# Moving the mode sums of a Fourier mixing to GpSimd, storing its modes in pairs, and asking for the next stage's first data before them

## The chip, the cores and the metric

The kernel runs on one core of one Trainium2 chip. The metric is the time that the device takes for one launch, in microseconds (us). The kernel before was run three times: 11272.87, 11274.17 and 11285.87 us, median 11274.17 us. A profiler recorded one more execution, whose own time was 11293.58 us.

A core has five engines that run at the same time, each through its own list of instructions: TensorE (PE, matrix products), VectorE (DVE), ScalarE (ACT), GpSimd (POOL) and SyncE (SP, which here only starts transfers). Sixteen DMA engines move data between the main memory (DRAM) and the on-chip memory (SBUF). PE writes its results to a second on-chip memory (PSUM). An instruction that needs the result of another engine or of a transfer waits for a semaphore, and everything behind it on its own engine waits with it.

## The reference

64 images of 256x256 points and 64 texts of 77x256 numbers are the inputs. A tokenizer made of four Fourier layers turns each image into 256x256 numbers, these 256 rows and the 77 text rows make 333 tokens, and a transformer block with a routed feed-forward part works on them. Cut to what matters here:

```python
h = concatenate([x, gx, gy]) ; v = h @ p_w + p_b            # 32 channels
for i in range(4):
    x_ft = rfft2(v)
    out1 = einsum('bixy,ioxy->boxy', x_ft[:, :, :12, :12],  W1)   # low modes
    out2 = einsum('bixy,ioxy->boxy', x_ft[:, :, -12:, :12], W2)   # mirrored low modes
    x1 = irfft2(out_ft holding out1 and out2)
    v = x1 + einsum('bcxy,cd->bdxy', v, w_w[i]) + w_b[i]
    v = (v - mean) * rsqrt(var + 1e-5) * bn_g[i] + bn_b[i]        # over images and points
    if i < 3: v = relu(v)
h = einsum('bcxy,cu->bxyu', v, q_w) + q_b                   # 256 x 256 per image
h = concatenate([h, txt])                                   # 333 tokens
h = h + attention(layernorm(h))
h = h + routed_ffn(layernorm(h))                            # the better half of the tokens
```

Only 24 x 12 complex modes of each channel are kept. The multiplication of these modes by W1 and W2 is called mixing below. The kernel takes the sum and the sum of squares for the normalisation from the modes, so it needs sums of products of modes over all images before it can scale anything.

## The kernel before, in words

The program goes through these stages, in the profile's time: the transform of the input (`forward_first`, to about 115 us), mixing 0 with its statistics, layer 0 (to about 2540), mixing 1 (its loop from about 2560 to 2606), layer 1, mixing 2, layer 2, mixing 3 (its loop ends at about 8645), and the transformer, image by image, to the end. The function `mix` (from L427) does a mixing and its statistics; `layer` (from L551) turns the mixed modes of every image back into points, adds the channel product, applies the normalisation and transforms the result forward again. The order in which a layer's steps are issued is written out by hand in `ORDER`: words such as `pre5` or `ld2@1`, where the number is the step's index and `@1` means that the step is done for one image ahead. Mixing and layers run under a manual schedule: each engine executes its instructions in the order in which the program issues them.

**Mixing.** The loop runs over 12 values of kp. Each step handles two of the 24 x-modes for all 64 images; the images lie on 64 partitions, twice (the two modes, kk = 0 and 1). PE makes 48 small products (L457) into a PSUM tile; ACT copies it out as `e` (L469). From `e`, ACT (L474, L475) and DVE (L476, L477) fill `ob`, one of three buffers of 128 partitions with the modes in the order in which they will be read; DVE copies a slice to `f0` (L478), forms combinations in `a_` (two L480), multiplies by `e` (L486) and adds the product to the accumulator `acc` (L487; the first step writes `acc` directly, L484). ACT makes two small copies of 64 partitions into `fr` (L494), which holds the modes in mirrored order. SP then stores each half of `ob` with a transfer of 512 KB over 64 partitions (L495) to `mix_d`, which in DRAM has the index order image, part, mode, channel: an image's modes are one contiguous piece.

**Statistics.** After the loop DVE reduces `acc` (L502 to L504), combines `fr` with `f0` (L505 to L507: difference, sum, product), reduces that (L508 to L511), PE sums over partitions (L513), and small operations, with a square root on ACT (L523), give the scale `s_` and the shift `t_` (L518 to L530).

**Start of a layer.** DVE prepares the constant rows of two tiles `ams` (L584, L590). SP then loads into them the mixed modes of the first two images (`load_am`, L623, four transfers). POOL multiplies them by the scale (`scale_am`, L631), PE expands them in x (L662), DVE transposes (L670), PE expands in y into `ring` (L682), and in layers 1 and 2 adds the channel product of the layer's input `vin` (L693), which SP loads in the steps `ld` (L656, two transfers of 512 KB per `vin`, four `vin` buffers). In layer 0 there is no `vin`: its input is the tile `mv`, which holds a grid, loaded by SP (L598, two transfers of 2 MB, each behind nothing but the stores of mixing 0), and rows of `x`, loaded by POOL (`load_x`, L638), which must come after the grid. In the program's order, `load_am` for two images comes first, then (in layer 0) the x loads, then `scale_am`, then the steps of `ORDER`, the first of which in layers 1 and 2 issue `ld`.

**Start of the transformer.** Constants come from a table (`cstt`, on SP's queue) and weights on ACT's queue (from L872: w1, w2, then the four attention weights). A few products of weights (L922 to L947) are made once. Then each image runs through `image_rows`: load the modes of the image (`am`), scale and reduce (L964, L968), expand (L970, L975), load the last layer's points in eight transfers of 1 MB (`ch`, pool `inp` of seven buffers) and reduce them over channels on PE (L982). This part is not under the manual schedule: a scheduler orders it, and may move it beside the end of mixing 3. The pool `inp` is made after the pool of constants, `tcon`.

Of the kernel before, what the change touches and what calls it, by code (L numbers as in the profile page):

```python
# [9 lines left out]
F32 = mybir.dt.float32  # L10
# [7 lines left out]
C = 32  # L18
M = 12
# [134 lines left out]
def tile_fno_fusion_transformer(ctx: ExitStack, tc: tile.TileContext, a, cst_d, grid_d, out):  # L154
# [27 lines left out]

    vd = [dram.tile([128, 8, 8, S], F32, name=f"v{b}_{n}") for n in range(2) for b in range(B)]
    vd = [vd[:B], vd[B:]]
    mix_d = [dram.tile([B, 2, KX, 32 * C], F32, name=f"mix{i}") for i in range(L)]
    xh_d = [dram.tile([128, B, 144], F32, name=f"xh{i}") for i in range(1, L)]

    flip = [0]
# [239 lines left out]
    def mix(i, lhs, wm, u2, spread):  # L428
# [5 lines left out]
        with tc.tile_pool(name="mo", bufs=1) as op, tc.tile_pool(name="me", bufs=3) as ep, \  # L434
# [13 lines left out]
            for kp in range(M):  # L448
# [19 lines left out]
                for hv in halves:  # L468
                    nc.scalar.copy(  # L469
                        e[hv].rearrange("p g q s o -> p q g (s o)"),  # L470
                        ps[hv, :, 0:384].rearrange("p q (g s) -> p q g s", g=3),
                    )
                    ev = e[hv].rearrange("p g q s o -> p (g q) s o")
                    nc.scalar.mul(o1[hv, 0], ev[:, :, 2, :], -1.0)  # L474
                    nc.scalar.copy(o1[hv, 1], ev[:, :, 1, :])  # L475
                    nc.vector.tensor_copy(o0[hv, 0], ev[:, :, 1, :])  # L476
                    nc.vector.tensor_copy(o0[hv, 1], ev[:, :, 2, :])  # L477
                    nc.vector.tensor_copy(f0[hv, kp], ev[:, 0, 1:3, :])  # L478
                    for n, (us, fs) in enumerate(((0, 1), (3, 2))):
                        nc.vector.scalar_tensor_tensor(  # L480
                            a_[hv, :, n, :], ev[:, :, us, :], 2.0, ev[:, :, fs, :], ALU.mult, ALU.add
                        )
                    if kp == 0:
                        nc.vector.tensor_mul(acc[hv], a_[hv], ev[:, :, 1:3, :])  # L484
                    else:
                        nc.vector.tensor_mul(a_[hv], a_[hv], ev[:, :, 1:3, :])  # L486
                        nc.vector.tensor_add(acc[hv], acc[hv], a_[hv])  # L487
                if kp == 0:
                    nc.vector.tensor_add(fin[0:B, 1, :], e[0:B, 0, 0, 1, :], e[0:B, 0, 0, 0, :])
                for kk in range(2):  # L490
                    to = (M - kp) % M if kk == 0 else M - 1 - kp
                    hv = slice(64 * kk, 64 * kk + B)
                    if kk or kp != M // 2:
                        nc.scalar.copy(fr[hv, to], e[hv, 0, 0, 1:3, :])  # L494
                    nc.sync.dma_start(  # L495
                        mix_d[i][:, :, 2 * kp + kk, :], ob[kp % NB][hv].rearrange("b p o k -> b p (o k)")
                    )
            for hv in halves:
                q = fin[hv, 0, :]
                t1 = op.tile([128, C], F32, name="t1", bufs=2)  # L500
                t2 = op.tile([128, C], F32, name="t2", bufs=2)
                nc.vector.reduce_sum(q, acc[hv].rearrange("p a s o -> p o (a s)"), axis=AX.X)  # L502
                nc.vector.tensor_add(t1[hv], acc[hv, 0, 0, :], acc[hv, 0, 1, :])
                nc.vector.scalar_tensor_tensor(q, q, 2.0, t1[hv], ALU.mult, ALU.subtract)  # L504
                nc.vector.tensor_sub(fr[hv, :, 0, :], fr[hv, :, 0, :], f0[hv, :, 0, :])  # L505
                nc.vector.tensor_add(fr[hv, :, 1, :], fr[hv, :, 1, :], f0[hv, :, 1, :])
                nc.vector.tensor_mul(fr[hv], fr[hv], f0[hv])  # L507
                nc.vector.reduce_sum(t1[hv], fr[hv, :, 0, :].rearrange("p a o -> p o a"), axis=AX.X)  # L508
                nc.vector.reduce_sum(t2[hv], fr[hv, :, 1, :].rearrange("p a o -> p o a"), axis=AX.X)
                nc.vector.tensor_sub(t1[hv], t1[hv], t2[hv])  # L510
                nc.vector.scalar_tensor_tensor(q, t1[hv], 0.5, q, ALU.mult, ALU.add)  # L511
# [34 lines left out]
    def layer(i, st, src, dst, acc):  # L546
# [7 lines left out]
        with ExitStack() as cx:  # L554
# [66 lines left out]
            def load_am(b):  # L621
                for n in range(2):
                    nc.sync.dma_start(  # L623
                        ams[b % 2][64 * n:64 * n + 2 * KX],
                        mix_d[i][b].rearrange("p k c -> (p k) c")[:, 512 * n:512 * n + 512],
                    )

            def scale_am(b):
# [21 lines left out]
                    load_x(b, n)  # L650

            def ld(b, t, e):
                vin[b, t] = ip.tile([128, 8, S], F32, name="vin")
                for n in range(2):
                    rows = slice(4 * n, 4 * n + 4)
                    nc.sync.dma_start(vin[b, t][:, rows], src[b][:, t, rows])  # L656
# [153 lines left out]
            for word in ORDER[min(i, 1)].split():  # L810
# [2 lines left out]
                name = word if word in run else word.rstrip("0123456789")  # L813
                steps.append((run[name], int(word[len(name):] or 0), e, int(late or 0)))

            for b in range(2):
                load_am(b)
            if i == 0:
# [42 lines left out]

    src = vd[L % 2]
    s_, t_ = st
    tcon = ctx.enter_context(tc.tile_pool(name="tcon", bufs=1))
    inp = ctx.enter_context(tc.tile_pool(name="inp", bufs=7))
    tabt = tables(tcon, "exT", "tri", "cstt")
    EXT, MASK4, IOTA = tabt("exT"), tabt("mask4"), tabt("iota")
    TRI = tabt("tri").rearrange("p (t j) -> p t j", t=3)
# [90 lines left out]

    def image_rows(b):  # L960
        am = ap_.tile([2 * KX, 32 * C], F32, name="am")
        nc.sync.dma_start(am, mix_d[L - 1][b].rearrange("p k c -> (p k) c"))
        tmp = am.rearrange("p (o k) -> p o k", k=32)
        nc.vector.tensor_tensor(  # L964
            tmp, tmp, qrow[0:2 * KX].to_broadcast([2 * KX, C, 32]), ALU.mult
# [268 lines left out]
```

## Time and profile before

| what | value |
|---|---|
| three runs, median | 11274.17 us |
| profiled execution, its own time | 11293.58 us |
| span of the profiled execution | 11291.7 us |
| busy share of the span: PE, DVE, ACT, POOL | 94%, 75%, 57%, 13% |
| transfers | 3457.29 MB, 306 GB/s mean |
| stores of modes (L495) | 96 of 512 KB, 5.6 us to landing (median) |
| loop of mixing 1, 2560 to 2604 us | DVE busy 41.86 us, ACT 39.35, PE 21.74, POOL 0 |

Busy times say how long an engine had an instruction in work, not whether the end of the program waited for it. For that the profile has a chain of waits: it starts from the last instruction and goes back, at each step, to what released it. A line of a group gives the line of the kernel, the engine, the operation, the tiles written and read with their shapes, then the count, total busy time and mean time of one, and then how long the engine stood idle before such instructions and what ended the wait. "issue" stands for time in which an engine waited for nothing that the profile shows.

### The profile page before, as it was taken

How to read it: one execution, taken by the hardware profiler on the slowest of the kernel's cores; microseconds unless marked ns; L12 is line 12 of the kernel's file. 1: busy time of each engine (PE TensorE's matmuls, PEld its weight loads, DVE VectorE, ACT ScalarE, POOL GpSimd, SP SyncE). 2: the span in 40 equal slices, each digit the busy share in tenths (PEclk: the TensorE clock that was granted, in tenths of full speed). 3: DMA queues.
4: the chain of work that ended last, by engine and by line, in shares of the span. 5: the costliest groups of instructions: out<-in, count | busy, mean ns of one | idle time of the engine just before them, and what ended most of it. 6: DMA issues, size and time to landing. Idle time of an engine off the chain costs nothing.

```text
span 11291.7 us, 409300 instructions
## 1 busy us (share of the span) xinstructions
PE 10625.0 (94%) x182550; PEld 5738.0 (51%) x182550; DVE 8446.5 (75%) x10381; ACT 6473.1 (57%) x10673; POOL 1442.4 (13%) x2179
## 2 busy tenths in 40 slices
PE   6999999998999999999799999999996999999999
PEld 3555555554444444444444444444443666666666
DVE  6888888887777777777677777777775666666665
ACT  5777777775566655566555566655563333333333
POOL 1111111110000000000000000000000333333333
PEclk8999999998999999999899999999998999999999
DMA  6776676678999999999899999999998555555553
GB/s 213 247 250 244 249 247 248 246 253 320 383 376 382 380 377 372 374 379 379 305 375 380 380 376 378 381 380 376 372 379 291 226 227 228 227 227 228 226 227 140
DMA packets 972544, 3457.29 MB, mean 306 GB/s; under 512 B 149784, under 2 KB 199320, under 8 KB 903832
## 3 DMA queue, kind: packets, MB, share of 16 engines
q1 hardware_dynamic: 905344, 3366.80, 77.8%
q0 software_dynamic: 58288, 60.60, 2.3%
q8 instruction: 1428, 23.40, 0.8%
q10 hardware_dynamic: 7144, 3.72, 0.1%
q14 instruction: 340, 2.79, 0.1%
HBM read 1733.60 MB, written 1696.92 MB: 304 GB/s over the span
## 4 chain that ended last, share of the span: by engine, by line
PE 62%; DMA 20%; DVE 9%; ACT 3%; issue 3%; SPq 2%; POOL 0%; ACTq 0%; DVEq 0%; POOLq 0%
PE ring L752 15%; DMA v<-vo 11%; PE ring L682 9%; PE ring L730 8%; DMA vin<-v 6%; PE ring L693 5%; PE hp L982 4%; PE ring L662 3%; PE pp L1145 3%; PE pp L1156 3%; PE ring L786 2%; DVE vo L707 2%; PE pp L1110 2%; PE pp L1175 2%; PE pp L1072 1%
## 5 line engine op out<-in xcount | busy, mean ns | idle before, releaser
L741 ACT ACTIVATE ring<-ring 128x1024 f32<-128x1024 f32 x3072 | 3115.8, 1014 | 1188.4 <-PE ring L730 1119.5
L719 DVE STREAM_TRANSPOSE t<-vo 128x2048 f32<-128x2048 f32 x1536 | 3465.7, 2286 | 20.9 <-DVE vo L707 0.9
L730 PE MATMUL ring<-vo,w 32*32 32x512 f32 x49152 | 2413.1, 600 | 85.0 <-ACT vo L705 68.3
L707 DVE TENSOR_SCALAR vo<-ring 128x1024 f32<-128x1024 f32 x1280 | 1544.5, 1221 | 1199.7 <-PE ring L693 806.6
L705 ACT ACTIVATE vo<-ring 128x1024 f32<-128x1024 f32 x1792 | 1791.7, 1023 | 1044.1 <-PE ring L693 500.9
L752 PE MATMUL ring<-t,cst 32*32 32x512 f32 x49152 | 2072.0, 599 | 51.0 <-issue 44.9
L752 PEld LDWEIGHTS ring<-t,cst 32*32 32x32 f32 x49152 | 913.4, 103 | 925.6 <-issue 622.6
L730 PEld LDWEIGHTS ring<-vo,w 32*32 32x32 f32 x49152 | 803.2, 103 | 1070.2 <-issue 407.1
L693 PE MATMUL ring<-vin,ws 32*32 32x512 f32 x32768 | 1287.8, 603 | 22.9 <-issue 16.2
L682 PE MATMUL ring<-cst,y 24*128 24x256 f32 x16384 | 1230.3, 402 | 77.0 <-DVE vo L707 61.7
L682 PEld LDWEIGHTS ring<-cst,y 24*128 24x128 f32 x16384 | 789.5, 185 | 993.2 <-DVE vo L707 392.4
L631 POOL TENSOR_TENSOR ams<-ams,bns 48x512 f32<-48x512 f32 x384 | 400.5, 1043 | 6989.4 <-DMA ams<-mix 6510.1
L670 DVE STREAM_TRANSPOSE y<-ring 128x1024 f32<-128x1024 f32 x384 | 763.1, 1987 | 329.5 <-PE ring L662 328.5
L682 PE MATMUL ring<-mv,y 29*128 29x256 f32 x8192 | 705.3, 403 | 36.3 <-ACT ring L741 19.6
L682 PEld LDWEIGHTS ring<-mv,y 29*128 29x128 f32 x8192 | 456.9, 185 | 369.0 <-ACT ring L741 209.3
L786 PEld LDWEIGHTS ring<-cst,zt 128*128 128x128 f32 x4608 | 533.6, 193 | 177.1 <-ACT vo L705 114.2
L762 ACT COPY half<-ring 128x1024 f32<-128x1024 f32 x192 | 194.4, 1013 | 731.4 <-PE ring L752 731.4
L1183 POOL DMA_DIRECT2D out_dram<-o x1024 | 508.2, 505 | 659.0 <-DVE o L1178 616.9
L741 ACT ACTIVATION_READ_ACCUMULATOR ring<-ring 128x1 f32 x3072 | 585.6, 191 | 0.0
L786 PE MATMUL ring<-cst,zt 128*128 128x96 f32 x4608 | 565.6, 280 | 6.1 <-DVE zt L770 5.7
L770 DVE STREAM_TRANSPOSE zt<-ring 128x1024 f32<-128x1024 f32 x192 | 377.4, 1965 | 248.1 <-PE ring L752 248.1
L662 PE MATMUL ring<-ams,cst 49*128 49x512 f32 (+1 forms) x1536 | 450.6, 642 | 99.1 <-POOL ams L631 37.2
(374 smaller groups left out, 9762.6 us busy)
## 6 DMA issues: line engine op xcount, KB each, us to landing
v<-vo SPq DMA_DIRECT2D x3072, 512.0 KB, 7.8
vin<-v SPq DMA_DIRECT2D x2048, 512.0 KB, 9.1
ch<-v SPq DMA_DIRECT2D x512, 1024.0 KB, 12.5
mix<-ob SPq DMA_DIRECT2D x96, 512.0 KB, 5.6
ams<-mix SPq DMA_DIRECT2D x384, 96.0 KB, 8.0
xin<-in_x_dram SPq DMA_DIRECT2D x16, 1024.0 KB, 6.5
mv<-in_x_dram POOLq DMA_DIRECT2D x256, 64.0 KB, 7.4
out_dram<-o POOLq DMA_DIRECT2D x1024, 16.0 KB, 3.0
```

The source lines that it names most:

```text
L662: nc.tensor.matmul(ps[:, n, :], lhsT=EX[hv, 128 * h:128 * h + 128], rhs=ams[b % 2][hv], start=True, stop=True, skip_group_check=True,)
L670: nc.vector.transpose(y_[b, h].rearrange("p q c -> p c q"), ring[key][0][1].rearrange("p n (c k) -> p (n c) k", k=32),)
L682: nc.tensor.matmul(ps[n][:, 256 * r:256 * r + 256], lhsT=y_[b, t // 4][32 * n:32 * n + K, q:q + 4, :].rearrange("p q c -> p (q c)"), rhs=m ...
L693: nc.tensor.matmul(ps[n][32 * j:32 * j + 32], lhsT=ws[32 * n:32 * n + 32], rhs=v[32 * n:32 * n + 32, 2 * j:2 * j + 2, :], start=False, sto ...
L705: nc.scalar.activation(to, ring[key][h][1], AF.Relu)
L707: nc.vector.tensor_scalar(to, ring[key][h][1], 0.0, None, ALU.max)
L719: nc.vector.transpose(t32[b, t // 2][:, :, 8 * (t % 2):8 * (t % 2) + 8, :].rearrange("p y s c -> p s y c"), vo[b, t].rearrange("p s (y l) ...
L730: nc.tensor.matmul(ps[n][32 * j:32 * j + 32], lhsT=w4[i + 1][32 * n:32 * n + 32], rhs=vo[b, t][32 * n:32 * n + 32, 2 * j:2 * j + 2, :], st ...
L741: nc.scalar.activation(ps, ps, AF.Square, accum_out=acc[:, at:at + 1])
L752: nc.tensor.matmul(ps[n][32 * j:32 * j + 32], lhsT=FYT[32 * n:32 * n + 32, k, :], rhs=t32[b, j][32 * n:32 * n + 32, k].rearrange("p s c -> ...
L786: nc.tensor.matmul(ps[:, 0, 96 * g:96 * g + 96], lhsT=zt_[:, h, k0:k0 + 4, :].rearrange("p k c -> p (k c)"), rhs=FX[:, h, 48 * r:48 * r + ...
L1183: nc.gpsimd.dma_start(out[b, 64 * n + 16 * g:64 * n + 16 * g + 16].rearrange("(p t) d -> p t d", t=2), o[32 * g + 8 * n:32 * g + 8 * n + 8 ...
```

## The change

Four things are changed.

1. In steps kp = 1 to 10 of each mixing, POOL instead of DVE adds the product to `acc`; step 11 stays on DVE. The small copies into `fr` go from ACT to POOL. After the loop, POOL instead of DVE does the difference, sum and product of `fr` and `f0`, and the program issues these ahead of DVE's reductions.
2. The modes of both halves are stored with one transfer of 1 MB over 128 partitions. For that, `mix_d` has the index order part, mode, image, channel: the rows of one image are now 256 KB apart. The loads of `ams` and `am` read them from there, in pieces of 2 KB and 4 KB.
3. A layer issues its first four `ld` steps (in layer 0 these don't exist) ahead of `load_am`; the step `ld` itself does nothing for a tile that is already asked for.
4. In the transformer the pool `inp` is made ahead of `tcon`, and with buffers tracked tile by tile.

In the compiled order this gives, on SP's queue: in mixings 1 and 2, eleven stores, two transfers of `vin`, the last store, six of `vin`, then the four loads of `ams`; in mixing 0, eleven stores, half of the grid, the last store, the other half, then `ams`; in mixing 3, eleven stores, `cstt`, the first `ch`, the last store, six `ch`, then the first `am`. On ACT's queue, the square root of mixing 3 (L523) stands between the issues of w1 and w2, and the four attention weights come behind both.

```diff
-    mix_d = [dram.tile([B, 2, KX, 32 * C], F32, name=f"mix{i}") for i in range(L)]
+    mix_d = [dram.tile([2, M, 2, B, 32 * C], F32, name=f"mix{i}") for i in range(L)]
...
                         nc.vector.tensor_mul(a_[hv], a_[hv], ev[:, :, 1:3, :])
-                        nc.vector.tensor_add(acc[hv], acc[hv], a_[hv])
+                        add = nc.gpsimd if kp < M - 1 else nc.vector
+                        add.tensor_add(acc[hv], acc[hv], a_[hv])
...
                     if kk or kp != M // 2:
-                        nc.scalar.copy(fr[hv, to], e[hv, 0, 0, 1:3, :])
+                        nc.gpsimd.tensor_copy(fr[hv, to], e[hv, 0, 0, 1:3, :])
+                for kk in range(1 if B == 64 else 2):
+                    hv = halves[kk]
+                    to = mix_d[i][:, kp] if B == 64 else mix_d[i][:, kp, kk:kk + 1]
                     nc.sync.dma_start(
-                        mix_d[i][:, :, 2 * kp + kk, :], ob[kp % NB][hv].rearrange("b p o k -> b p (o k)")
+                        to.rearrange("p k b c -> (k b) p c"), ob[kp % NB][hv].rearrange("b p o k -> b p (o k)")
                     )
             for hv in halves:
+                nc.gpsimd.tensor_sub(fr[hv, :, 0, :], fr[hv, :, 0, :], f0[hv, :, 0, :])
+                nc.gpsimd.tensor_add(fr[hv, :, 1, :], fr[hv, :, 1, :], f0[hv, :, 1, :])
+                nc.gpsimd.tensor_mul(fr[hv], fr[hv], f0[hv])
...
-                nc.vector.tensor_sub(fr[hv, :, 0, :], fr[hv, :, 0, :], f0[hv, :, 0, :])
-                nc.vector.tensor_add(fr[hv, :, 1, :], fr[hv, :, 1, :], f0[hv, :, 1, :])
-                nc.vector.tensor_mul(fr[hv], fr[hv], f0[hv])
...
-                        mix_d[i][b].rearrange("p k c -> (p k) c")[:, 512 * n:512 * n + 512],
+                        mix_d[i][:, :, :, b].rearrange("p m k c -> (p m k) c")[:, 512 * n:512 * n + 512],
...
             def ld(b, t, e):
+                if (b, t) in vin:
+                    return
...
+            first = [
+                (b + late, n) for b in range(-2, 2) for f, n, _, late in steps if f is ld and 0 <= b + late < B
+            ]
+            for b, n in first[:4]:
+                ld(b, n, None)
             for b in range(2):
                 load_am(b)
...
+    inp = ctx.enter_context(tc.tile_pool(name="inp", bufs=7, reuse_waits="tile"))
     tcon = ctx.enter_context(tc.tile_pool(name="tcon", bufs=1))
-    inp = ctx.enter_context(tc.tile_pool(name="inp", bufs=7))
...
-        nc.sync.dma_start(am, mix_d[L - 1][b].rearrange("p k c -> (p k) c"))
+        nc.sync.dma_start(am, mix_d[L - 1][:, :, :, b].rearrange("p m k c -> (p m k) c"))
```

## The prediction

> **What bounds the kernel now.** The change touches the four mixing stages and the hand-over from each to the next stage, so I looked at the page's summary first only to size these, then at busy times by stretch, at the groups of the second mixing (`mix` with i = 1), and at the chain of waits around each hand-over.
>
> From the view of stretches (columns: engine busy time and instruction count, granted PE clock, share of the DMA engines, GB/s):
>
> ```profile
> 120.00:165.00 45.00, 22.26 (x982) 18.91 (x981) 43.16 (x85) 40.80 (x60) 6.00 (x3) 0.72 0.86 257
> 2560.00:2604.00 44.00, 21.74 (x1024) 20.08 (x1023) 41.86 (x83) 39.35 (x59) 0.00 (x0) 0.77 0.89 258
> 2604.00:2632.00 28.00, 10.49 (x86) 4.52 (x102) 14.06 (x32) 1.35 (x2) 4.16 (x4) 0.50 0.64 222
> 5000.00:5045.00 45.00, 44.27 (x948) 21.76 (x952) 34.76 (x20) 28.12 (x46) 2.09 (x2) 1.00 1.00 384
> ```
>
> After window and length stand PE, PE loads, DVE, ACT and POOL. In a mixing loop (rows 1 and 2) DVE is busy 42 of 44 us, ACT 39, POOL nothing (in the first row three memsets), so DVE bounds it, with ACT close. Layers 1 and 2 (row 4) have DMA at 1.00. Four mixings of some 60 us are 2% of the program: nothing in this change can move the total by more than a per cent unless it touches the layers.
>
> Groups of the second mixing's loop, twelve steps of kp in 44 us (busy us, mean ns):
>
> ```profile
> L469 ACT COPY e<-mps 128x1536 f32<-128x1536 f32 x12 | 17.3, 1441 | 3.8 <-PE mps L457 3.6
> L494 ACT COPY fr<-e 64x64 f32<-64x64 f32 x23 | 5.9, 255 | 0.2
> L486 DVE TENSOR_TENSOR a__31813<-a__31813,e 128x768 f32<-128x768 f32 x1 | 1.0, 959 | 0.0
> L487 DVE TENSOR_TENSOR acc<-acc,a__31813 128x768 f32<-128x768 f32 x1 | 1.0, 959 | 0.0
> ```
>
> A step takes 3.67 us. DVE's starts are spaced 0.45+0.33+0.09 (L476 to L478), 1.04 (two L480), 1.0 (L486), 0.87 (L487).
>
> The chain of waits at the end of that loop (start, length, what):
>
> ```profile
> 2604.59 0.97 DVE acc L487
> 2605.58 1.44 DVE fin L502
> ...
> 2608.31 0.97 DVE fr L507
> ...
> 2611.06 0.20 DVE fin L511
> ...
> 2616.78 2.15 DMA ams<-mix
> ...
> 2619.10 1.05 POOL ams L631
> ```
>
> So 5.7 us of reductions and products, then statistics, then `ams`: all serial, no other work covers it. In the first hand-over something else ends last:
>
> ```profile
> 167.71 18.94 DMA mv<-in_grid_dram
> ...
> 189.60 1.07 POOL ams L631
> ```
>
> L631 waits for POOL's x loads (L638), which wait for the grid; the modes, asked for at 182.51, needed 2.2 us and had been there about 4.8 us. Into the transformer the chain is a row of loads:
>
> ```profile
> 8642.43 14.14 DMA w<-in_L_ffn_w_dram
> ...
> 8656.65 5.12 DMA cstt<-in_cst_dram
> ...
> 8682.47 7.91 DMA ch<-v
> ```
>
> **Does GpSimd run beside DVE?** This decides, and the loop before shows no such pair. The transformer does. In order of time, with POOL adding 128x256 tiles:
>
> ```profile
> 8733.99 2.56 POOL L1171 TENSOR_TENSOR h<-h,fz 128x256 f32<-128x256 f32 x3 [33.13 <-DVE fz L1004]
> 8734.88 0.41 DVE L1026 SCALAR_TENSOR_TENSOR junk<-fz,wrB 128x256 f32<-128x256 f32 x1
> 8735.33 0.62 DVE L1030 TENSOR_SCALAR dg<-cst,wcol 128x128 f32<-128x128 f32 x1
> 8735.88 0.96 DVE L1026 SCALAR_TENSOR_TENSOR junk<-fz,wrB 128x256 f32<-128x256 f32 x1
> ```
>
> The same L1026 takes 0.41 and 0.96. Instruction by instruction, the second add (8734.77 to 8735.87, 1.10 instead of 0.72) lay over DVE's first, and DVE's second L1026 ended only 0.29 after POOL's third add. L1030 is 0.286 alone and 0.62 here. They take turns.
>
> **The Trainium skill.** "SBUF — State Buffer", section "Who interferes with whom": DVE and GpSimd share a port pair under an exclusive lock; a DVE operation with two SBUF inputs, or a copy in a two-port mode, contends with GpSimd reading SBUF; a `tensor_reduce` doesn't. The trace agrees (0.41 to 0.96). All DVE operations of a step but the reductions have such operands: L480, L486 and L487 read two SBUF inputs, and L477 does 384 elements in 0.33 where the two-input L480 needs 0.52, so it is in a fast copy mode. "GPSIMD Engine Reference", section "3.1 Elementwise — side-by-side cycle accounting" prices a two-input add of 2048 elements at 4497 ns against 2293 on DVE; for 768 elements an estimate from it is 1.69 us. From the trace: 0.716 for 256, 1.04 for 512 (L631), by that slope 1.37 for 768. I take 1.6. "SBUF — State Buffer", section "Can I just issue two DMAs to hit both halves?" says that only a transfer over 128 partitions reaches all 16 ports; the stores before have 64 partitions and land in 5.6 us, but no trace of a 128-partition one of this shape exists here. At a share of 0.86 to 0.89 the stores don't set the loop's end, so I price this at nothing; the cover is gone if the step falls below about 3.2 us.
>
> **Part 1, sums to GpSimd (kp 1 to 10).** Removed from DVE: 0.87 a step. Left 2.8. Added on POOL: 1.6. If they take turns, a step is 2.8+1.6 = 4.4 instead of 3.67: +0.7, ten times, +7 us per mixing. Ends: the lock might cover only part of an add (0.57 of 0.72 by the times above), so 1.37 x 0.8 = 1.1, a step of 3.9, +2; or 1.8 plus two small copies, 4.9, +12. The `fr` copies (L494) leave ACT, 0.49 a step, which gains nothing while DVE sets the pace; on POOL they stand behind the add of their step and hold up only the next add.
>
> **Part 2, the end.** L505 to L507 (1.9 us between L504 and L508) leave DVE's chain. On POOL they are 0.85+0.85+1.6 = 3.3, behind the add of kp 10 and four copies, and in turns with DVE's kp 11. From the end of kp 10's L486 to L511: before 10.4 us. After: POOL 1.6+0.3+3.3 and DVE 2.8+0.9 in turns, 8.9; L502 can lie beside; then L508 to L511, 1.9, and 0.4 for L503 and L504: 11.2. So +1, between -2 and +3. Per mixing +8.
>
> **Part 3, early loads.** Mixing 0: grid and x no longer end last. `ams` is asked for 8 later, 190.5, there at 192.7; the grid was there at 186.7, is queued about a kp earlier behind the last stores, so about 190, and x adds 2.2: L631 near 192.9 instead of 189.6, +3.3. SP's order is 11 stores, one grid half, store 12, the other half, then `ams`. On POOL the x loads now stand behind the products at the end of the mixing, which end near 180, before the grid is there. Mixing 1 and 2: two vin transfers before the last store, six after it, then `ams`. The first L693 (2627.39) waited for no vin before, so only queueing behind 4.2 MB is saved: -1 (0 to -2); +7 each. ams and vin on SP cost 0.45 an issue, all long before the statistics end. Mixing 3: `cstt` and ch0 before the last store, six more ch behind it. The chain ran through w (14.14), cstt (5.12) and ch (7.91). The weights (ACT's queue) still have to come, and now share the bandwidth with 7 MB of ch; from 8641 to 8693 16.5 MB went at 318 GB/s mean where 384 is sustained, worth up to 9 us. On ACT, w2 and the attention weights are issued only behind the square root (L523), which waits for the statistics, now 8 later; hence not the whole 9. I take -7 (-3 to -12): +1 net.
>
> **Part 4, layout.** A mode row of one image now lies 256 KB from the next instead of behind it; pieces stay 2 KB for the layers. Priced at nothing: layer 0 and the transformer are bound by PE; layers 1 and 2 have no such cover.
>
> Sum: 3.3+7+7+1 = +18 us. The profiled execution, 11,293.58 us with a span of 11,291.7, would become 11,312. It lies 19.4 above the median of the runs, 11,274.17; on that scale 11,292.
>
> **Rivals.**
> A, taking turns (above): +18, 11,292; own range 11,276 to 11,310. For: L1026 and L1030. Against: no 768-element add was seen.
> B, GpSimd runs beside DVE: a step then falls to ACT's 3.28-0.49 = 2.8, or 2.9 with its waits. Ten steps -7.7, the end -2.5. Mixing 0 gains only 5 (the grid is bound by DMA), mixings 1 and 2 11 each, mixing 3 10 and 3: -40, 11,234. For: two of three transformer adds ran at full speed. It decides once a step goes below 3.67, that is if an add blocks DVE for less than 0.9 us. This is the other side.
> C, PE sets the pace: its matmul bursts start on an "issue" gap, about 3.7 us a step. The loop stays, the hand-overs gain 5+1+1+7, the end some 1.5 each: -20, 11,254.
> D, the strided mode rows cost the DMA-bound layers: 192 KB of 16.8 MB per image is 1.1% of 45.2 us, 0.5 us; doubled, 0.5 x 128 images = +65 on A, 11,357. It decides against any gain from a fifth more per row. The transfers may also not be faster and the early loads merely crowd the weights out, which is A's upper end.
>
> **Chances.** A 0.59, B 0.25, C 0.09, D 0.07. A change of less than 0.2% (22.5 us) can about not be told from none by a measurement of this kernel. A puts 0.37 within it, 0.20 above (step of 4.6 or more, or less won at the transformer), 0.02 below; B 0.25 faster; C splits 0.05 and 0.04; D slower. Faster 0.31, same 0.42, slower 0.27. The range leaves out D and the far half of B: 11,228 to 11,325.
>
> **What would show it.** A: L480, L486 or L476 with means above their 0.55, 0.96, 0.54 in the loop, an L487 successor on POOL of 1.4 to 2.5 us, mixing 1 from first to last step some 7 us longer. B: DVE means unchanged and steps near 2.9. Hand-over 0: L631 released by the modes, not the x loads. Transformer: no 7.9 us wait for ch. D: images of layer 1 longer than 45.2 us. The prediction falls if DVE's operations keep their length, or if the weights or the first chunks move the transformer's start by more than 12 us.

## The result, and the profile after

The changed kernel is slower: median 11298.26 us against 11275.06 us, each of 20 runs, so +23.2 us; the ratio is 1.0019 with a 95% interval of 1.0012 to 1.0025. The profiled execution has a span of 11304.7 us against 11291.7, only 13.0 us more, because the layers vary by themselves. From the first L662 of a layer to the first L476 of the next mixing, layer 1 took 2961.4 us in the profiled execution before and 2945.8 in the one after, layer 0 2369.8 and 2374.6, layer 2 2955.4 and 2958.1. Over all profiles of this study layers 1 and 2 vary from 2945.7 to 2961.4. So the stages around the mixings are compared one by one.

Here is how the time divides, from the starts and ends of instructions in the two traces (us; "last statistics step" is L511 before and L515 after):

| stretch | mixing 0 | 1 | 2 | 3 |
|---|---|---|---|---|
| first to last L476 of the loop (eleven steps), before | 41.16 | 41.21 | 40.90 | 40.95 |
| after | 46.00 | 45.32 | 45.37 | 45.15 |
| last L476 to last statistics step, before | 9.45 | 9.52 | 9.45 | 9.91 |
| after | 11.17 | 11.23 | 11.23 | 11.23 |
| last statistics step to first L662 (L668 after), before | 18.24 | 8.94 | 8.94 | |
| after | 18.33 | 8.80 | 8.74 | |
| last statistics step to the second image's h, before | | | | 80.30 |
| after | | | | 80.37 |

The loops lose 4.1 to 4.8 us each and the ends of the mixings 1.3 to 1.8: 24 us in all, about the measured loss. The hand-overs, for which the early loads were, give nothing.

The second mixing's loop in the view of stretches (window, length, PE, PE loads, DVE, ACT, POOL, granted PE clock, DMA share, GB/s) is still full of DVE; POOL is now busy 28 of 44 us, and the DMA engines are at 0.62 where they were at 0.89:

```profile
2570.00:2614.00 44.00, 22.18 (x1011) 19.99 (x999) 43.34 (x66) 34.66 (x35) 28.04 (x28) 0.76 0.62 242
```

Its groups (busy us, mean ns, idle before and releaser) show which operation grew. L477, 540 ns before, takes 1456; the sum on POOL takes 1804. First the line of the kernel before, then those of the changed one:

```profile
L477 DVE COPY ob<-e 128x384 f32<-128x384 f32 x12 | 6.5, 540 | 0.0
```

```profile
L469 ACT COPY e<-mps 128x1536 f32<-128x1536 f32 x12 | 17.6, 1469 | 8.0 <-POOL fr L495 7.4 <-PE mps L457 0.6
L477 DVE COPY ob<-e 128x384 f32<-128x384 f32 x12 | 17.5, 1456 | 0.0
L495 POOL COPY fr<-e 64x64 f32<-64x64 f32 x23 | 13.3, 579 | 6.4 <-ACT e L469 5.7
L488 POOL TENSOR_TENSOR acc<-acc,a__32050 128x768 f32<-128x768 f32 x1 | 1.8, 1804 | 1.6 <-DVE a__32050 L486 1.6
```

The instructions of one step in order of time (start, length, engine, line):

```profile
2610.86 0.49 DVE L476 COPY ob<-e 128x384 f32<-128x384 f32 x1
2611.09 1.81 POOL L488 TENSOR_TENSOR acc<-acc,a__31986 128x768 f32<-128x768 f32 x1 [1.55 <-DVE a__31986 L486]
2611.19 2.07 DVE L477 COPY ob<-e 128x384 f32<-128x384 f32 x1
2612.85 1.00 POOL L495 COPY fr<-e 64x64 f32<-64x64 f32 x2
2613.21 1.05 DVE L480 SCALAR_TENSOR_TENSOR a__32050<-e 128x384 f32<-128x384 f32 x2
```

POOL's sum starts while L476 is on DVE, and L477, next in line, ends at 2613.26, 0.36 us after POOL's sum (2612.90). In the kernel before only 0.33 us lie between its start and that of the next operation, so it did its work after the sum. The two L480 beside POOL's copies keep their length. The step is 4.31 us, against 3.75 in the mean of the eleven before.

The chain of waits at the end of that loop:

```profile
2615.40 1.80 POOL acc L488
...
2618.70 0.97 POOL fr L495
2619.66 0.96 DVE acc L488
2620.65 1.46 DVE fin L509
...
2622.51 1.85 DVE fin L511
...
2624.46 0.80 DVE t L512
...
2626.21 0.20 DVE fin L515
```

L511, 0.19 us long before (as L504), is drawn out to 1.85 by POOL's product L505 (2622.50 to 2624.30), and the reduction L512 can only begin when that product is there. The reduction L509 keeps its length (1.46 us; 1.44 before, as L502) beside POOL's difference and sum. In the last step the sum of kp 10 (2615.40) holds up L477 as well, which takes 2.06 us there. So the end is 1.7 us longer, although 1.9 us of work were taken off DVE.

The first hand-over, and the start of the transformer, in the chain of waits:

```profile
168.64 22.60 DMA mv<-in_grid_dram
...
194.11 1.07 POOL ams L635
```

```profile
8648.76 10.07 DMA ch<-v
...
8659.25 3.34 DMA b2c<-in_L_ffn_b_dram
...
8665.87 5.33 ACTq L928
...
8673.75 7.85 DMA won<-in_L_attn_Wo_dram
...
8682.17 0.68 PE wtp L933 x2
...
8704.20 6.27 DMA ch<-v
```

The second half of the grid was asked for 3.5 us earlier than before, counted from the last statistics step (8.25 us ahead of its end instead of 4.76), but took 22.60 us instead of 18.94.

In the transformer the loads of ACT's queue now stand in the chain: the first product of weights (L933) starts 21.3 us after the last statistics step, against 14.8 before. The requests on SP's queue in order of time show that the early loads were hardly early:

```profile
8648.76 0.82 SPq L991 DMA_DIRECT2D ch<-v  x1
8652.02 0.37 SPq L499 DMA_DIRECT2D mix<-ob  x1
8661.17 18.40 SPq L991 DMA_DIRECT2D ch<-v  x6
```

One `ch` was asked for ahead of the statistics, which end at 8660.84; the next six follow from 8661.17 on. By the trace's semaphore events, requests on both queues wait for an earlier transfer that uses the same semaphore: the second `ch` for a small load of ACT's queue, and that queue's load of boB (a bias, L910) for the first `ch`. So ACT's small loads went out late, and w1 behind them only at 8660.77; before, w1 was asked for 5.4 us ahead of the statistics' end. Then wrB, wq, wk and wv (L922, L928) took 10.6 us to be issued, 3.2 before; what lengthens these issues isn't shown.

### The profile page after: what moved, and what is told of

Its sections match the earlier page's. It is cut to its first block, busy times and chain, and to the rows that moved or that the text cites. A ratio compares the mean times of both kernels' runs of the same rounds, so it can differ in the third digit from the quotient of the medians.

```text
span 11304.7 us, 409305 instructions
## 1 busy us (share of the span) xinstructions
PE 10604.6 (94%) x182550; PEld 5726.8 (51%) x182550; DVE 8475.5 (75%) x10329; ACT 6453.2 (57%) x10581; POOL 1583.9 (14%) x2323
## 4 chain that ended last, share of the span: by engine, by line
PE 61%; DMA 21%; DVE 9%; ACT 3%; issue 3%; SPq 2%; POOL 0%; ACTq 0%; DVEq 0%; POOLq 0%
PE ring L758 15%; DMA v<-vo 12%; PE ring L688 9%; PE ring L736 8%; DMA vin<-v 6%; PE ring L699 5%; PE hp L993 4%; PE ring L668 3%; PE pp L1156 3%; PE pp L1167 3%; PE ring L792 2%; PE pp L1121 2%; DVE vo L713 2%; PE pp L1186 2%; PE pp L1083 1%
## 5 line engine op out<-in xcount | busy, mean ns | idle before, releaser
L668 PE MATMUL ring<-ams,cst 49*128 49x512 f32 (+1 forms) x1536 | 451.8, 643 | 105.6 <-POOL ams L635 37.1
```

Source lines behind the costliest of these rows:

```text
L668: nc.tensor.matmul(ps[:, n, :], lhsT=EX[hv, 128 * h:128 * h + 128], rhs=ams[b % 2][hv], start=True, stop=True, skip_group_check=True,)
```

## The experiments

The recorded expectations don't count the copy of experiment 4: what they call the fourth to the tenth experiment is 5 to 11 here.

Two theories of the loop were set against each other. Theory 1: POOL's sum and DVE's operations take turns at SBUF. Theory 2: ACT's L469 waits for POOL's mirrored copies, since these hold `e`; the groups above show this wait, 7.4 us.

**1. The sums alone.**

```diff
 kernel before
-                        nc.vector.tensor_add(acc[hv], acc[hv], a_[hv])
+                        add = nc.gpsimd if kp < M - 1 else nc.vector
+                        add.tensor_add(acc[hv], acc[hv], a_[hv])
```

> The kernel before with one edit: the sums of kp 1 to 10 on GpSimd (stores, mirrored copies, end of the mixing and early loads as before). Theory 1, turns: GpSimd's add (1.80 us in the changed kernel) keeps DVE's fast copies and two-input operations out, most of all L477; then eleven steps of a mixing loop take 45 to 46 us as in the changed kernel (45.2 to 46.0) instead of 41, L477 stays near 1.4 us instead of 0.54, and the program is 18 to 24 us slower than before. Theory 2, release of e: in the changed kernel ACT's L469 waits for the mirrored copies on GpSimd, which stand behind the add and hold a buffer of e; with those copies back on ACT the steps return to 3.75 or less (41 us), and the program is within 5 us of before.

Ratio to before 1.0018 (1.0011 to 1.0025). Eleven steps: 45.42, 45.30, 45.17, 45.23 us. The groups of the second loop:

```profile
L477 DVE COPY ob<-e 128x384 f32<-128x384 f32 x12 | 20.5, 1708 | 0.0
L469 ACT COPY e<-mps 128x1536 f32<-128x1536 f32 x12 | 17.3, 1441 | 2.8 <-PE mps L457 2.5
```

L469 no longer waits for the copies, and the loop is as slow as in the changed kernel. Theory 2 falls: that wait was real and cost nothing. The whole loss of the change is in this one edit; the last stretch of the mixing is longer with it alone too (11.1 us).

**2. The mirrored copies alone.**

```diff
 kernel before
-                        nc.scalar.copy(fr[hv, to], e[hv, 0, 0, 1:3, :])
+                        nc.gpsimd.tensor_copy(fr[hv, to], e[hv, 0, 0, 1:3, :])
```

> The kernel before with one edit: the mirrored copies (fr) on GpSimd instead of ACT. Theory 1: a copy of 64 elements reads SBUF for too short a time to keep DVE out; eleven steps 39.5 to 42 us, DVE means unchanged within 0.1 us. Theory 2: without an add ahead of them the copies don't hold e for long; also 39.5 to 42. Tells only what the copies alone cost; over 43 would say that they block DVE too.

Eleven steps: 41.64, 40.86, 40.61, 41.68 us; in the second loop DVE's means are within 0.04 us of before. The one run gave 11276.53 us, within the spread of the kernel before (11269.25 to 11296.69). On POOL such a copy takes 0.59 to 0.78 us in the mean of a loop, against ACT's 0.255. The shortest take 0.23 us, and the long ones lie beside DVE's operations, which keep their length: here it seems to be POOL that waits.

**3. A fill in the place of the sum.**

```diff
 changed kernel
-                        add = nc.gpsimd if kp < M - 1 else nc.vector
-                        add.tensor_add(acc[hv], acc[hv], a_[hv])
+                        if kp < M - 1:
+                            nc.gpsimd.memset(scr, 0.0)       # scr: 128 x 1976
+                        else:
+                            nc.vector.tensor_add(acc[hv], acc[hv], a_[hv])
```

> The changed kernel, but GpSimd fills a scratch tile of 128x1976 with zeros instead of each sum of kp 1 to 10 (near 1.8 us, as long as the add; it reads nothing, and no longer waits for DVE). The sums of kp 1 to 10 are left out, so the statistics are not those of the reference. Theory 1, in the form that the reading of SBUF is what keeps DVE out: L477 back to 0.54 and eleven steps 30 to 37 us; in the form that any use of the shared ports does: L476 or L477 still above 1 us, steps 38 to 45. Theory 2, GpSimd's own chain sets the pace through e: its work per step is the same 1.8 + 1.0, L469 still waits for the mirrored copies; it could hold steps at 2.9 at most when the add no longer waits for L486, so DVE means are what decides: unchanged from before under theory 2 whatever GpSimd runs.

The sums are left out, so the statistics are not those of the reference. The one run took 11267.80 us; eleven steps: 36.93, 36.65, 34.10, 38.78 us. In the second loop (lines are one further down here; L489 is POOL's fill, L477 and L478 are DVE's two copies into `ob`):

```profile
L489 POOL MEMSET scr<- 128x1976 f32 x10 | 17.5, 1750 | 0.6
L477 DVE COPY ob<-e 128x384 f32<-128x384 f32 x12 | 7.7, 645 | 6.7 <-ACT e L470 6.3
L478 DVE COPY ob<-e 128x384 f32<-128x384 f32 x12 | 6.4, 535 | 0.0
```

POOL was about as busy as with the sum. Beside the fill DVE's two-input operations keep their length: L487, which lies under it in nearly every step, takes 0.96 us. L478 hardly meets a fill. L477, the first of the two copies, does, and it isn't spared (start, length, engine, line):

```profile
2574.56 1.75 POOL L489 MEMSET scr<- 128x1976 f32 x1
2574.95 0.96 DVE L487 TENSOR_TENSOR a__31669<-a__31669,e 128x768 f32<-128x768 f32 x1
2575.84 0.87 DVE L477 COPY ob<-e 128x384 f32<-128x384 f32 x1
```

This copy ends 0.40 us after the fill (2576.31). In the four loops 20 of the 48 L477 start while a fill runs, and every one of them ends 0.35 to 0.51 us after the fill's end; the longest takes 1.95 us. So a fill keeps out this copy too, but not DVE's two-input operations, and each of the two forms of theory 1 holds in part. It costs little here because most of it lies beside those: DVE's operations from L477 to L487 take 0.1 to 0.3 us a step more than in the kernel before (kp 1 to 10, 3.48 to 3.61 us against 3.26 to 3.36).

One of four loops was over the 37 us expected. DVE waits for `e` here, so with less on DVE something else sets the pace, at 3.1 to 3.5 us a step.

**4. A copy in the place of the sum.**

```diff
 third experiment
-                            nc.gpsimd.memset(scr, 0.0)
+                            nc.gpsimd.tensor_copy(scr, scs)  # both 128 x 1792
```

> The third experiment with a copy from one scratch tile to another, 128x1792, near 1.8 us, in the place of the fill: GpSimd now reads SBUF with one input for the whole time, and again waits for nothing of DVE's; the sums of kp 1 to 10 are left out. If reading is what keeps DVE out, DVE's copies and two-input operations grow as with the add: 1.2 to 1.6 us more per step over L477, L478, L481 and L487, eleven steps 42 to 46 us. If it takes two inputs on GpSimd's side, they stay as with the fill (0.65, 0.54, 0.61, 1.02) and eleven steps take 34 to 39 us.

Here too the sums are left out. The one run took 11314.44 us; eleven steps: 47.74, 45.34, 45.48, 44.93 us, the first above the 46 expected. In the second loop (L491 is POOL's copy; L480 is DVE's second copy into `ob`, L489 DVE's product):

```profile
L491 POOL COPY scr<-scs 128x1792 f32<-128x1792 f32 x10 | 20.0, 2004 | 0.6
L480 DVE COPY ob<-e 128x384 f32<-128x384 f32 x12 | 11.1, 927 | 0.0
L489 DVE TENSOR_TENSOR a__31609<-a__31609,e 128x768 f32<-128x768 f32 x1 | 2.3, 2325 | 0.0
```

POOL's copy, which takes 1.83 us at the shortest and waits for no DVE result, makes DVE's operations 1.3 to 1.6 us a step longer than in the kernel before; the fill of 1.75 us made them 0.1 to 0.3 longer. It need not be a sum: one input is enough. What the reading adds is that two-input operations are kept out as well. As POOL's copy isn't tied to L486 here, it falls on other operations as well (a product of 2.3 us instead of 0.96).

**5. No GpSimd: the new stores and the early loads alone.** The changed kernel with sums, mirrored copies and products back on DVE and ACT, as they were.

> The changed kernel with the sums, the mirrored copies and the end of the mixing back on DVE and ACT: what stays is the 128-partition store with its layout and the early loads. If the prediction's part 3 holds (mixing 0 -5, mixings 1 and 2 -1 each, transformer -7), it is 10 to 18 us faster than before, ratio near 0.9988. If the early loads gain nothing, as the changed kernel's stages suggest (from the first L476 of mixing 3 to the second image's h 5.6 us longer, no more than its loop), within 5 us of before. In both cases eleven steps take 41 us again, or less if the new stores had mattered.

Ratio 0.9995 (0.9987 to 1.0003): the same as before. Eleven steps 40.75 to 41.17 us. Last statistics step to first L667 (the former L662): 18.6 us in the first hand-over, no better than 18.24, and 9.49 and 10.28 in the next two, worse than 8.94: asked for behind eight transfers of `vin`, the modes took 2.77 and 3.54 us to land instead of 2.15. From the last statistics step to the second image's h 81.9 against 80.3. The chain at the transformer:

```profile
8619.41 10.19 DMA ch<-v
8629.62 4.50 DMA boB<-in_L_attn_bo_dram
...
8644.91 7.73 DMA won<-in_L_attn_Wo_dram
...
8653.20 0.67 PE wtp L932 x2
```

Wo was asked for 14.3 us after the last statistics step; before the change it was 5.1.

**6. The sums back on DVE, the rest of the change kept.**

```diff
 changed kernel
-                        add = nc.gpsimd if kp < M - 1 else nc.vector
-                        add.tensor_add(acc[hv], acc[hv], a_[hv])
+                        nc.vector.tensor_add(acc[hv], acc[hv], a_[hv])
```

> The changed kernel with the sums of kp 1 to 10 back on DVE; mirrored copies and the products at the end of the mixing stay on GpSimd. If the sums alone cost the time (theory 1), eleven steps take 40 to 42 us again and the program is 18 to 26 us faster than the changed kernel, 0 to 8 slower or faster than before. The end, from the last L476 to the end of the last statistics step, 9.45 before and 11.2 after: 8 to 9.5 if the late sum of kp 10 and the blocked L477 had made it long; 10.5 or more if the products on GpSimd (0.99, 0.99 and 1.80 us in the changed kernel, in line behind the last mirrored copy) are themselves what the reductions wait for.

Ratio 0.9999 (0.999 to 1.0007); eleven steps 41.70, 40.70, 40.78, 40.89 us. The end is 13.89, 10.54, 10.53 and 10.58 us: over the 9.45 to 9.91 of before. So the products on POOL by themselves cost 0.7 to 1.1 us at the end of a mixing, and 4.4 in the first, where POOL asks for x, and waits for the grid, ahead of the last product. With the sum of kp 10 on POOL the end was 11.1 us without them (experiment 1); the two costs don't add up, and together they make 11.2.

**7. Weights before w1 and w2, and x behind the scaling.** In the fifth experiment's kernel, w1, w2 and wrB are asked for after the four attention weights, and:

```diff
-            if i == 0:
-                for b in range(2):
-                    for n in range(4):
-                        load_x(b, n)
             for b in range(2):
                 scale_am(b)
+            if i == 0:
+                for b in range(2):
+                    for n in range(4):
+                        load_x(b, n)
```

> The kernel of the fourth experiment (128-partition stores and early loads, nothing on GpSimd) with two edits. First, ACT asks for the four attention weights ahead of w1, w2 and wrB. If late weights ate the gain of the early loads at the transformer (Wo asked for 14.3 us after the last statistics step, with ch loads ahead; first product of weights 22.5 us after it, before the change 14.8), that product comes 8 us or more earlier and the second image's h 5 to 10 us earlier, counted from the first L476 of mixing 3 (131 us in both kernels). If the transformer's start is set by the volume of data, 16.5 MB, the second h stays within 3 us. Second, in layer 0 GpSimd scales the first modes before it asks for x, for both images. If the x loads (many small pieces) crowd out the second half of the grid, its landing comes down from 22.6 us to under 17; if not, it stays. The first L662 then follows the modes at once, some 5 us earlier, but the first products with mv wait for x.

Ratio 0.9996 (0.9988 to 1.0005). The small loads ahead of the weights were still issued up to 2.9 us apart, since several of them wait for an earlier transfer that uses the same semaphore; the first product came 15.3 us after the last statistics step, 7.3 earlier than in experiment 5, and the second h 3.4 us earlier: the first just short of the 8 expected, the second between the two expectations. The chain of the first hand-over:

```profile
183.21 2.13 DMA ams<-mix
185.50 1.04 POOL ams L634
...
190.46 7.74 DMA mv<-in_x_dram
198.24 1.88 PE ring L687 x3
```

With the x loads out of the way the modes landed in 2.13 us and L634 began 4.1 us earlier than L631 before; but then PE waits for x, until 198.24, where before it began L682 at 195.89. Whether x crowds out the grid shows in the traffic after the request for its second half (at 165.17 in experiment 5, at 165.06 here; columns as above). First experiment 5, then this one:

```profile
177.00:180.00 3.00, 0.00 (x0) 0.00 (x0) 2.85 (x11) 0.00 (x0) 0.00 (x0) 0.50 1.14 141
180.00:183.00 3.00, 0.00 (x0) 0.00 (x0) 2.86 (x5) 0.00 (x0) 0.00 (x0) 0.50 1.07 160
```

```profile
177.00:180.00 3.00, 0.00 (x0) 0.00 (x0) 2.85 (x10) 0.00 (x0) 0.00 (x0) 0.50 0.58 236
180.00:183.00 3.00, 0.00 (x0) 0.00 (x0) 2.86 (x5) 0.00 (x0) 0.00 (x0) 0.50 0.00 0
```

Without x nothing is left to move at 180: the second half landed in less than 15 us. With x on its way it took 22.61, with the DMA engines full at 141 to 160 GB/s. So x does crowd it out; the 17 us expected for this case held.

**8. The same, by halves, on the kernel before.** Weights ahead of w1 and w2; x of the first image before the scaling, x of the second behind it.

> The kernel before with two edits, meant as a faster version: the four attention weights asked for ahead of w1, w2 and wrB, and in layer 0 GpSimd scales the modes of the first two images between the x loads of the first and of the second. L631 starts when the modes have landed, 4.5 us earlier than before, and nothing of the first image waits for the second half of the grid: layer 0 begins 4 to 5 us earlier. Transformer: before the change cstt ended last (8661.78), not the weights, so 0 to 5 us there. Together 4 to 10 us faster than before, 0.9991 to 0.9996.

Ratio 0.9995 (0.9986 to 1.0003): no gain. Here L631 waits for the modes themselves:

```profile
181.88 7.83 DMA ams<-mix
```

Asked for while grid and x are on their way, they take 7.83 us, not 2.13. In the kernel before they took 5.65 (182.51 to 188.16). In the transformer the first product of weights came 5.4 us after the statistics instead of 14.8, but the first `ch` was asked for 9.5 us later, and the second h came only 2.4 us earlier.

**9. The weights at the very front.** In the fifth experiment's kernel ACT asks for wq, wk, wv and wo first, then for the small loads, then for w1, w2 and wrB (cut to the order of the requests):

```diff
+            # at the head of ACT's loads for the transformer
+            nc.scalar.dma_start(wn[n], a[f"L0_attn_W{n}"].rearrange("(h p) d -> p h d", p=128))
...
+        nc.scalar.dma_start(hbias, a["L0_tok_q_b"].partition_broadcast(128))
+        # bq, bv, bvE, wvE, boB, b2c, brB, b1c, w1, w2, wrB follow, then hbias is finished
```

> The kernel of the fourth experiment (128-partition stores, early loads, nothing on GpSimd); ACT asks for the four attention weights ahead of all other loads of the transformer, the small ones too. In the sixth experiment the small loads still stood ahead of the weights and were issued one by one, up to 10 us apart, while the first ch was on its way. If that queue behind ch is what takes the gain of the early loads, Wo is now asked for before the first ch or right after it, the first product of weights starts at most 12 us after the last statistics step (22.5 in the fourth experiment, 14.8 before), and the second image's h comes 8 to 15 us earlier than in the fourth, counted from the first L476 of mixing 3 (132.1), so 117 to 124. If volume sets it, 128 or more.

Ratio 0.9986 (0.9979 to 0.9992), 11268.24 us. Wo was asked for 14.8 us ahead of the last statistics step, the first product of weights comes 1.3 us after it, and the second h 124.2 us after the first L476 of mixing 3, 7.9 less than in experiment 5: just short of what was expected. With the eleventh image it is 13.1 us ahead of the kernel before (465.1 against 478.2). Its chain shows what is left:

```profile
8625.67 7.31 DMA bvc<-in_L_attn_bv_dram
...
8651.64 5.81 DMA am<-mix
...
8667.77 8.44 DMA ch<-v
```

A DVE operation on bv (`bvr`) now stands in DVE's order ahead of the last statistics and holds them up by 4 us. No run has the weights in front without the early loads, so the part of each in this gain isn't shown.

**10. Work taken from DVE to ACT.** The kernel before with the mirrored copies on GpSimd, and

```diff
-                    nc.vector.tensor_copy(o0[hv, 0], ev[:, :, 1, :])
+                    nc.scalar.copy(o0[hv, 0, 6:], ev[:, 6:, 1, :])
+                    nc.vector.tensor_copy(o0[hv, 0, 0:6], ev[:, 0:6, 1, :])
...
-                    nc.vector.tensor_copy(f0[hv, kp], ev[:, 0, 1:3, :])
+                    nc.scalar.copy(f0[hv, kp], ev[:, 0, 1:3, :])
```

> The kernel before; the mirrored copies on GpSimd (single-input, 64 elements, which did not slow DVE in the second experiment), and with the time that this frees on ACT, ACT takes from DVE half of L476's copy and the copy to f0 (L478). DVE loses 0.17 + 0.09 us a step, ACT loses 0.49 and gains about 0.45 + 0.25. If DVE sets the pace of the loop, a step falls from 3.72 to 3.45 to 3.55 and eleven steps to 38 to 39 us; four loops give 8 to 12 us, ratio 0.9989 to 0.9993. If PE's gaps set it (rival C of the prediction), eleven steps stay at 40.5 to 41.5.

Ratio 0.9998 (0.9989 to 1.0006); eleven steps 43.43, 40.37, 39.74, 41.78 us. A miss: the relief of DVE didn't reach the time.

**11. Experiments 9 and 10 together.**

> Both of the last two together: a version that leaves the sums on DVE and keeps the new stores and the early loads. Sum of the two: 16 to 25 us faster than before, ratio 0.9978 to 0.9986; within 5 us if neither works.

Ratio 0.9981 (0.9973 to 0.9989), 11260.12 us: the lowest ratio of the study; the changed kernel is at 1.0019. Eleven steps 38.62 to 38.84 us, in all four loops, which neither half had.

**12. Experiment 10 with the new stores.** To find out which part of the eleventh made the loops even, only the 128-partition stores and their layout were added to the tenth.

> The ninth experiment (mirrored copies on GpSimd, half of L476 and L478 on ACT, nothing else moved) with the 128-partition stores and their layout, without the early loads. In the tenth, where stores, early loads and weights in front were all there, every loop's eleven steps took 38.6 to 38.8 us; in the ninth 39.7 to 43.4, with PE standing idle for 14 to 20 us in gaps within a loop instead of 11 to 14. If the stores make the difference (they use the DMA engines less), eleven steps take 38.5 to 39.2 here in mixings 0 to 2. If the early loads do, they stay at 39.7 to 43.4.

Ratio 0.9985 (0.9978 to 0.9992); eleven steps 38.80, 38.86, 38.89, 38.82 us. It is the stores. The second loop in the view of stretches, and PE's groups there, of experiment 10 (first in each pair of views) and of this one:

```profile
2568.35:2608.72 40.37, 22.42 (x1014) 20.36 (x999) 37.40 (x66) 37.46 (x56) 11.27 (x22) 0.82 0.90 266
L457 PE MATMUL mps<-wm,xh 32*64 32x128 f32 x511 | 21.7, 362 | 14.6 <-issue 12.9 <-ACT e L469 1.7
```

```profile
2557.40:2596.26 38.86, 22.71 (x1023) 19.78 (x1023) 37.37 (x67) 38.39 (x57) 13.74 (x23) 0.88 0.74 289
L457 PE MATMUL mps<-wm,xh 32*64 32x128 f32 x511 | 20.6, 339 | 10.8 <-ACT e L469 5.7 <-issue 4.9
```

The old stores keep the DMA engines 0.90 busy for 266 GB/s, the new ones 0.74 for 289; and PE's idle time in gaps that the profile calls "issue" falls from 12.9 to 4.9 us. What PE waits for in these gaps isn't shown. The profile lists transfers of a kind "instruction" among the queues, and gaps that shrink when the DMA engines have room would fit them; that was not tested.

## Why the prediction was right or wrong, point by point

**The total and its cause were right.** Forecast +18 with "within 0.2%" the likeliest; measured +23.2 at a ratio of 1.0019, at the edge of that. The prediction held that such a change can about not be told from none; with 20 runs each it can, since the interval (1.0012 to 1.0025) leaves out 1. Rival A, taking turns, is what happens, shown by experiments 1, 3 and 4 together.

**Part 1, loop.** Forecast a step of 4.4 and +7 us per mixing; measured a step of 4.31 once the loop runs evenly, and +4.1 to +4.8 over eleven steps, since the first steps are shorter and the step before was 3.75, not 3.67. Two terms were mis-sized and cancelled in part: POOL's sum is 1.80 us, not 1.6 (the estimate from the Trainium skill, "GPSIMD Engine Reference", section "3.1 Elementwise — side-by-side cycle accounting", 1.69, was nearer than the slope of 1.37), but its first 0.26 us lie beside L476 in the step shown, so DVE loses about 1.4 a step (kp 1 to 10: 4.69 to 4.78 us from L476 to L486, against 3.26 to 3.36). L477, which the list of signs left out, takes nearly all of it. L476 is hit once in three of the loops, L480 and L486 once each in the second. Each mirrored copy was put at about 0.15 us, and takes 0.58; it costs nothing, as forecast.

**Part 2, end.** Forecast +1, measured +1.3 to +1.8, in the range given. The turns work as described, and L502 could lie beside POOL's work, as said. L505 drew out L511 and held L512; the sum of kp 10 held L477. The sum alone makes the end 1.2 to 1.6 us longer (experiment 1), the products alone 0.7 to 1.1 (experiment 6).

**Part 3 was wrong; this is the step that failed.** Three terms, -4.7, -2 and -7, were all about zero.
Mixing 0: the prediction let the second half of the grid land about as much earlier as it was asked for. It was asked for 3.5 us earlier, counted from the statistics, and took 3.7 us longer, since the x loads run beside it: 22.6 us with them, less than 15 without (experiment 7). "The modes ... needed 2.2 us and had been there about 4.8 us" was misread as well: the 2.2 us were taken from the other hand-overs, and with grid and x on their way the modes took 5.65 us in the kernel before and 7.83 in experiment 8. In the kernel before they had been there for 1.4 us.
Mixings 1 and 2: the -1 each was 0.1 to 0.2, the near end of its range; in experiment 5, where the statistics come no later than before, the `vin` ahead of the modes cost 0.6 and 1.3 us.
Transformer: "six more ch behind it" was an order, not a time. One `ch` was asked for ahead of the statistics, the other six from 0.3 to 18.3 us after their end, because SP's and ACT's queues wait for each other's transfers. The working saw that w2 and the attention weights come behind L523, but took 3 us off for it. The small loads of ACT's queue, none of which was priced, then waited one after the other for earlier transfers, a ch of 1 MB in flight for 10 us among them, and Wo was asked for 12.9 us after the statistics (5.1 before). Of the 7.9 us wait for ch, 6.3 are left. Experiment 9 fits this: with the weights in front of the same early loads the second image comes 8 us earlier.

**Part 4, layout.** Nothing, as forecast: layers 1 and 2 took 2946.4 to 2961.4 us with the old layout and 2945.7 to 2959.0 with the new one, 2952 and 2951 in the mean, so rival D falls. The lower DMA share of the new stores fits what the Trainium skill says on ports ("SBUF — State Buffer", section "Can I just issue two DMAs to hit both halves?"). In the changed kernel the stores had the cover that was named, a step above 3.2 us, but that threshold was too low: at 3.5 they are already worth 0.9 to 4.6 us a loop (experiments 10 and 12).

**Rival B**, the other side, needed an add that blocks DVE for less than 0.9 us; it blocks 1.4. It also claimed too much: with little contention (experiment 3) a step is 3.1 to 3.5, not 2.9. **Rival C** didn't decide here, but the chain of experiment 10's second loop runs through PE's gaps (2.08 us from 2575.74, 2.44 from 2581.05).

That the sum came out so near was partly luck: a term too large in the loops (+32 in all with the ends, 24 measured) stood against gains of 14 that didn't come.

## What to carry to other kernels

Before moving elementwise work from a full DVE to an idle GpSimd, count it as time on the same engine: what DVE gives up (0.87 us here) has to be more than what GpSimd's longer operation keeps it from (1.4 of 1.80). A fill cost less (0.1 to 0.3 a step), as far as it lay beside DVE's two-input operations. An early load is only early if it is also issued early, and if nothing that is needed sooner has to be issued behind it: look at every queue whose loads share semaphores with it, and ask for what the first computation needs before the bulk. Transfers that don't set the end can still be worth widening, once the engine in front of them gets faster.

## What the runs showed of the hardware that was not expected

A fill on GpSimd of 1.75 us left DVE's two-input products at 0.96 us, but its first copy of 128x384 into `ob`, where it started during a fill, ended 0.35 to 0.51 us after the fill's end in all 20 cases; a GpSimd copy with a single input also drew out those products, to 2.3 us. A GpSimd copy of 64 elements on 64 partitions takes 0.23 to 1.0 us, 0.58 in the mean of the loop shown, against 0.255 on ACT. Small x loads on GpSimd's queue, 0.5 MB in all, made a grid load of 2 MB take 22.6 us instead of less than 15. Stores of 1 MB over 128 partitions landed in 4.7 us (median), those of 512 KB over 64 in 5.6. Stores of the same data over 128 instead of 64 partitions took 0.74 of the DMA engines' time at 289 GB/s instead of 0.90 at 266, and PE's gaps in front of its bursts of matmuls shrank with them.
